# Scores of a four-layer recurrent block: three bfloat16 parts on 72 rows, loaded by head from DRAM, in place of float32 products over 128 rows

## The chip, the cores and the metric

The kernel runs on one core of a Trainium2 chip. A core has five engines that run side by side, each with its own list of instructions: TensorE (PE in the profile; its weight loads are listed apart as PEld), VectorE (DVE), ScalarE (ACT), GpSimd (POOL) and SyncE (SP), which here issues every DMA. PSUM takes the products of TensorE, SBUF holds all else on the core, DRAM lies outside. The metric is the device time of one execution in microseconds; less is better. Three runs of the kernel before took 4462.1, 4463.2 and 4484.0 us; the median is 4463.2.

## What is computed

Eight rows (batch entries) of 512 positions by 128 channels pass through four layers. Each layer is a mixing part times a gated part, added to the row. The change touches the mixing part of the last layer alone, attention with 16 heads of 8 channels, of which each query keeps its 25 strongest keys:

```python
q = _layernorm(q, q_gamma, q_beta)
k = _layernorm(k, k_gamma, k_beta)
scores = jnp.einsum('bhnd,bhmd->bhnm', q, k) / jnp.sqrt(jnp.float32(D))
aw = jax.nn.softmax(scores, axis=-1)
topk = max(1, int(N * TOPK_RATIO))          # 25 of 512
kth = jax.lax.top_k(aw, topk)[0][..., -1:]
aws = aw * (aw >= kth).astype(aw.dtype)
aws = aws / (aws.sum(-1, keepdims=True) + 1e-08)
o_s = jnp.einsum('bhnm,bhmd->bhnd', aws, v)
...
o = a * o_s + (1.0 - a) * o_l               # o_l: a linear attention over softmax(q), softmax(k)
```

## The kernel before

**Recording and planning.** The kernel does not issue its instructions as it runs through its Python code. Every call is recorded as an `Op` on a `Tape`, with what it reads and writes. When all is recorded, `Tape.order` plans: it keeps a free time for each engine and an estimated cost for each operation (`Op.cost`), and at each step takes the operation that can start first, or, of several, the one with the longest way to the end behind it (`way`). Element-wise operations recorded for POOL may be planned on DVE or the other way round, and copies recorded for ACT on DVE. `Tape.play` then issues everything in the planned order, and each engine works through its list strictly in that order. That is why the profile puts nearly all instructions on line 467. Where the plan leaves TensorE idle, it puts filler: products of zeros into the PSUM tile `nd` (line 452). Filler is issued only in states of `nd` in which it does no harm. TensorE's clock is granted by the chip and is part of the plan (`Clock`).

**Streams.** Four streams of work run over the eight rows and are interleaved: `front` (layers 0 and 1, lane A of buffers), `middle` (layer 2 and the preparation of layer 3, lane B), `find` and `weigh` (layer 3, lane C). Row b's `find` is recorded about two row periods after its `front`. In the profile a tile carries its lane's letter: `midC` is a 128x512 buffer of lane C.

**Preparation** (`Layer3.channels`). Queries and keys of a row are normalised by head and transposed, so that channels lie on partitions. The channels are stored in such an order that eight small DMAs for q and eight for k, of 32 KB each, put the heads into `qh` (128 x 4 x 512) and `kh` (128 x 2 x 512). In both, a head has eight rows of channels and a ninth: −1 in `kh`, and in `qh` zero at first (eight more DMAs from a tile of zeros) and later the query's bound. There are two pairs of `qh` and `kh`, so row b waits until row b − 2 is done.

**First pass** (`find`, `rank`). For each of 4 tiles of 128 queries and each of 16 heads, one float32 product gives 128 x 512 scores in the single PSUM bank `sc`. The weights of that product are `only_q`: a copy of a 32-row strip of `qh` into a tile that is zero elsewhere, so that the product over 128 rows adds up one head only. Four such copies (ACT) are made for every eight heads. DVE then finds the 32 largest of each row of scores in four rounds: `max` gives the 8 largest, `match_replace` takes them out. After the first round the scores are in an SBUF tile `rest` (a `midC` buffer), and the next three rounds of a tile are recorded behind the first round of the following one. ACT exponentiates what is left and sums it.

**Bounds** (`bound`). After two tiles, a half of the queries, the 25th and 26th score give each query's bound between them; it is transposed (`cT`) and written to the ninth rows of `qh` by eight DMAs.

**Second pass** (`weigh`). For a half (256 queries), 4 blocks of 128 keys and 16 heads, a float32 product of `only_k` (strips of `kh`, copied as above) and `qh` gives scores minus the bound, transposed. ACT turns what is negative into minus infinity (Prelu with a slope of 1e30) and exponentiates; a product with `vpad` (values, and ones for the sums) accumulates in `nd`. `combine` divides, adds the linear attention and writes the row's output.

Of the kernel before, what the change touches and what calls it, by code (L numbers as in the profile page):

```python
# [17 lines left out]
P = 128  # L18
# [10 lines left out]
TOPK_ROUNDS = 3  # L29
# [11 lines left out]
    FILL | {AF.Exp, AF.Tanh, AF.Prelu, AF.Square, AF.Abs},  # L41
# [24 lines left out]
class View:  # L66
# [47 lines left out]
    def box(self):  # L114

        if self.room.pool.space == bass.MemoryType.DRAM:
            return 0, P, 0, 1 << 30
        whole = View.shadows[tuple(self.room.shape)]
        first = self.at.__array_interface__["data"][0] - whole.__array_interface__["data"][0]
        row = int(np.prod(self.room.shape[1:]))  # L120
        p0, f0 = divmod(first, row)
        span = [(s * (n - 1), s) for n, s in zip(self.at.shape, self.at.strides)]
        return p0, p0 + sum(d for d, s in span if s >= row) // row, f0, f0 + sum(d for d, s in span if s < row)
# [10 lines left out]
class Op:  # L134
# [29 lines left out]
    def cost(self, engine):  # L164
# [5 lines left out]
        if engine == "tensor":  # L170
            out, stay, move = wrote[0], read[0], read[1]
            passes = 2 if stay.room.dtype == F32 else 1
# [12 lines left out]
        if engine == "sync":  # L185
            size = 4 * int(np.prod((wrote or read)[0].shape))
            return 400.0, 1300.0 + size / 175.0
# [60 lines left out]
class Tape:  # L248
# [188 lines left out]
    def play(self):  # L437
# [11 lines left out]
        for n in self.order():  # L449
# [12 lines left out]
            if any(v.room.key == key for v in wrote):  # L462
                state = 2 if op.kw["stop"] else 1
            elif any(v.room.key == key for v in read):
                state = 0
# [72 lines left out]
class Lane:  # L538
# [35 lines left out]
    def tile(self, name, shape, bufs=1):  # L574
        return self.pool.tile(list(shape), F32, tag=name + self.lane, name=name, bufs=bufs)

    def scratch(self, name, shape):
        return self.dram.tile(list(shape), F32, tag=name, name=name)
# [96 lines left out]
def together(*parts):  # L675
# [10 lines left out]
    return got  # L686

# [531 lines left out]
class Layer3:  # L1219
# [17 lines left out]
    def __init__(self, k):  # L1237
# [17 lines left out]
        self.rows, self.heads = [], []  # L1255
        for i in range(2):
            qh, kh = core.held(f"qh{i}", (P, 4, T)), core.held(f"kh{i}", (P, 2, T))
            nc.gpsimd.memset(qh, 0.0)
            nc.gpsimd.memset(kh, -1.0)
            self.heads.append((qh, kh))  # L1260
        self.only_q, self.only_k = [], []
        for to, name in ((self.only_q, "q0"), (self.only_q, "q1"), (self.only_k, "k")):
            t = core.held(f"only_{name}", (P, 4, 2, P))
            nc.gpsimd.memset(t, 0.0)
            to.append(t)
        self.Wproj = core.whole("w3p")("Wproj")

    def row(self, b):

        r = Layer3.__new__(Layer3)  # L1270
        r.__dict__.update(self.__dict__)
        r.b, r.done, r.masses = b, False, {}
        self.rows.append(r)
        return r
# [17 lines left out]
    def channels(self, k, w, xn):  # L1292
# [35 lines left out]
        heads_of = lambda t: t.rearrange("p (r d s) -> p r s d", r=8, d=D)  # L1328
        for c, name in ((0, "q"), (1, "k")):
            for t in range(NT):  # L1330
                yield
                y = raw[:, t, c * P : (c + 1) * P].rearrange("p (r s d) -> p r s d", r=8, d=D)
                vec = lambda n: row(name + n).unsqueeze(1).unsqueeze(1).to_broadcast([P, 8, 2, D])
# [6 lines left out]
        for g in range(G):  # L1340
            yield
            mine = top[:, g, :].rearrange("p (r s) -> p r s", r=8)
            nc.vector.reduce_max(mine, heads_of(QK[:, g, :]), axis=AX.X)
            nc.gpsimd.tensor_sub(
                f[:, g, :].rearrange("p (r s d) -> p r s d", r=8, d=D),
                heads_of(QK[:, g, :]),
                mine.unsqueeze(3).to_broadcast([P, 8, 2, D]),
# [8 lines left out]
        while self.b >= 2 and not self.rows[self.b - 2].done:  # L1356
            yield
        self.qh, self.kh = self.heads[self.b % 2]
        for c in range(2):
# [4 lines left out]
            zs = k.mid("qk_t")  # L1364
            nc.scalar.copy(zs, z)
            for r in range(4):
                for i in range(2):
                    at = slice(32 * r + 9 * i, 32 * r + 9 * i + D)
                    to = self.kh[at, :, :] if c else self.qh[at, 2 * i : 2 * i + 2, :]
                    nc.sync.dma_start(out=to, in_=zs[32 * r + 16 * i : 32 * r + 16 * i + 16, :])  # L1370
                    if c == 0:
                        at = slice(at.stop, at.stop + 1)
                        none = self.only_q[0][P - 1 :, 0, 0:1, :].to_broadcast([1, 8, P])
                        nc.sync.dma_start(
                            out=self.qh[at, 2 * i : 2 * i + 2, :].rearrange(
                                "p s (t n) -> p (s t) n", n=P
                            ),
                            in_=none,
                        )
# [25 lines left out]

    def find(self):
# [5 lines left out]
        for n in range(NT * H):  # L1412
            t, h = divmod(n, H)
            a, r = divmod(h, 4)
            i, s = divmod(a, 2)
            if h == 0:
                top = k.tile("top", (P, H, (TOPK_ROUNDS + 1) * 8), 2)

                each = k.tile("each", (P, 2, H), 2)
            if h % 8 == 0:  # L1420
                only = self.only_q[i]
                for at in (slice(32 * j, 32 * j + 32) for j in range(4)):
                    nc.scalar.copy(
                        only[at, at.start // 32],
                        self.qh[at, 2 * i : 2 * i + 2, t * P : (t + 1) * P],
                    )
            z = k.psum.tile([P, T], F32, tag="sc", name="sc", bufs=1)
            k.mm(z, only[:, r, s, :], self.kh[:, s, :])
            head = 4 * r + a
            mine = top[:, head, :]  # L1430
            nc.vector.max(mine[:, 0:8], z)
            rest = k.mid("rest")
            nc.vector.match_replace(rest, mine[:, 0:8], z, -3e38)
            nc.gpsimd.tensor_scalar_mul(each[:, 0, head : head + 1], mine[:, 0:1], -self.scale)
            if behind:
                self.rank(*behind)
            behind = n, head, top, each, rest
            yield
        self.rank(*behind)

    def rank(self, n, head, top, each, rest):
        k, nc, H = self.k, self.k.nc, self.H
        mine = top[:, head, :]
        for m in range(1, TOPK_ROUNDS + 1):
            best = mine[:, 8 * m : 8 * m + 8]
            nc.vector.max(best, rest)
            if m < TOPK_ROUNDS:
                nc.vector.match_replace(rest, best, rest, -3e38)
        k.act(
            rest, rest, AF.Exp, scale=self.scale,  # L1450
            bias=each[:, 0, head : head + 1], accum_out=each[:, 1, head : head + 1],
        )
        t, h = divmod(n, H)
        if h < H - 1:
            return

        large = 8 * TOPK_ROUNDS
        e_top = k.tile("exp_top", (P, H, large))
        nc.gpsimd.tensor_sub(e_top, top[:, :, 0:large], top[:, :, 0:1].to_broadcast([P, H, large]))
        k.act(e_top, e_top, AF.Exp, scale=self.scale)  # L1460
        if t % 2 == 0:
            self.marks = k.tile("marks", (P, 4, 2, H), 2)
        nc.vector.reduce_sum(self.marks[:, 3, t % 2, :], e_top, axis=AX.X)
        nc.vector.tensor_add(self.marks[:, 3, t % 2, :], self.marks[:, 3, t % 2, :], each[:, 1, :])
        for to, at in enumerate((0, 24, 25)):
            nc.gpsimd.tensor_copy(self.marks[:, to, t % 2, :], top[:, :, at])
        if t % 2:
            self.bound(t // 2)

    def bound(self, half):  # L1470
# [4 lines left out]
        m, t25, t26, mass = (self.marks[:, i] for i in range(4))  # L1475
# [20 lines left out]
        cols = slice(half * self.HALF, (half + 1) * self.HALF)  # L1496
        for r in range(4):
            for i in range(2):
                at = 32 * r + 9 * i + D
                nc.sync.dma_start(  # L1500
                    out=self.qh[at : at + 1, 2 * i : 2 * i + 2, cols],
                    in_=cT[4 * r + 2 * i : 4 * r + 2 * i + 2, 0 : self.HALF],
                )
        self.bounded = half + 1

    def weigh(self, half, out):
# [18 lines left out]
        for n in range(32):  # L1525
            c, a, lo = n // 8, n // 2 % 4, 2 * (n % 2)
            i, s = divmod(a, 2)
            if n % 8 == 0:
                only = self.only_k[0]
                for at in (slice(32 * j, 32 * j + 32) for j in range(4)):  # L1530
                    nc.scalar.copy(only[at, at.start // 32], self.kh[at, :, c * P : (c + 1) * P])

            e = k.tile("weights", (P, 2, self.HALF), 3)
            z = k.ps().rearrange("p (j q) -> p j q", j=2)
            for j in range(2):
                k.mm(z[:, j, :], only[:, lo + j, s, :], self.qh[:, a, cols])
            k.act(e, z, AF.Prelu, alpha=1e30)
            k.act(e, e, AF.Exp, scale=self.scale)
            for j in range(2):
                r = lo + j  # L1540
                k.mm(
                    nd[32 * r : 32 * r + 32, i, :], self.vpad[:, c, 2 * r + i, s, :], e[:, j, :],
                    start=False, stop=n >= 30,
# [320 lines left out]
```

## Time and profile before

| | us |
|---|---|
| three runs | 4462.1, 4463.2, 4484.0 |
| median | 4463.2 |
| profiled execution, first to last instruction | 4466.0 |
| VectorE busy in it | 3883.5 |
| TensorE busy, with 689.5 of filler (L452) | 4215.7 |
| mean granted TensorE clock | 0.962 of full speed |
| DMAs issued by SP, all engines' queues | 100560 packets, 239.16 MB, 18.1% of 16 engines |

How to read the profile's lines. A row of the groups gives line, engine, operation, written tile <- read tiles, shapes and count, then busy time in us, the mean duration of one in ns, and idle time just before them with what ended it. Busy time counts overlapping records once, so busy time divided by the count can be less than the mean. A float32 product shows as two matmul records. A row of the stages gives a stretch, its length, and for each engine the busy time and, in brackets, the number of instructions, then the granted clock, the share of the DMA engines and GB/s. A row of the waits gives who waited for whom, the total in us, how often, and the longest.

### The profile page before, as it was taken

The numbers are of one execution on the slowest core, as the hardware profiler recorded it, in microseconds if no ns is written. First come the engines' busy times: TensorE is split into PE (matmuls) and PEld (weight loads), VectorE is DVE, ScalarE is ACT, GpSimd is POOL, SyncE is SP. The second block draws the span as 40 slices with busy tenths as digits, with TensorE's granted clock in tenths as the row PEclk, the third lists the DMA queues.
The fourth block names the chain that finished last, engine by engine and source line by source line (L and its number), as shares of the span: only waits on it lengthen the run. The fifth ranks groups of instructions, "written<-read, shape, count | busy, mean of one in ns | idle before, by whom it ended". The sixth has DMA issues, their size and how long they took to land. (4 is left out here: it accounts for less than half of the span.)

```text
span 4466.0 us, 59645 instructions
## 1 busy us (share of the span) xinstructions
PE 4215.7 (94%) x19508; PEld 2096.0 (47%) x19508; DVE 3883.5 (87%) x7617; ACT 2873.1 (64%) x5883; POOL 2492.4 (56%) x2973
## 2 busy tenths in 40 slices
PE   9998899999999999999999999999999999999699
PEld 4554454445444545444445445444444444444244
DVE  5438859989989998999898999999799989999894
ACT  3434455557766786767776686767775687375355
POOL 4117736873869565874757656784479533833010
PEclk9989999999999999999999999999999999999799
DMA  3122312221122121222012220221212100200000
GB/s 94 49 54 73 93 48 66 73 87 57 52 64 84 49 55 41 77 61 77 30 50 67 71 62 29 72 83 36 60 51 84 49 23 28 74 19 17 2 5 10
DMA packets 100872, 242.97 MB, mean 54 GB/s; under 512 B 13009, under 2 KB 25425, under 8 KB 96465
## 3 DMA queue, kind: packets, MB, share of 16 engines
q1 hardware_dynamic: 100560, 239.16, 18.1%
q8 instruction: 154, 2.52, 0.2%
q14 instruction: 158, 1.29, 0.1%
HBM read 206.60 MB, written 15.20 MB: 50 GB/s over the span
## 5 line engine op out<-in xcount | busy, mean ns | idle before, releaser
L467 DVE MAX8 topC<-midC 128x8 f32<-128x512 f32 x1374 | 912.8, 683 | 2.8
L467 POOL TENSOR_TENSOR midB<-midB,midB 128x512 f32<-128x512 f32 x520 | 670.7, 1299 | 104.4 <-DVE midB L467 94.3
L452 PE MATMUL nd<-ones,zeros 128*128 128x512 bf16 (+3 forms) x2956 | 689.5, 367 | 18.2 <-ACT midC L467 16.5
L467 PE MATMUL sc<-kh,only_q 128*128 128x512 f32 x1024 | 567.4, 637 | 66.4 <-DVE midC L467 22.4
L467 DVE MATCH_REPLACE8 midC<-topC,midC 128x512 f32<-128x512 f32 x916 | 619.5, 678 | 0.0
L467 PE MATMUL psA<-midA,wA 128*128 128x512 f32 (+3 forms) x986 | 524.5, 635 | 29.8 <-ACT midA L467 6.1
L467 PE MATMUL psC<-qh,only_k 128*128 128x256 f32 x1836 | 522.1, 397 | 16.5 <-ACT weightsC L467 10.8
L452 PEld LDWEIGHTS <-zeros 128*128 128x128 bf16 x2956 | 282.6, 100 | 458.8 <-issue 217.0
L467 ACT ACTIVATE midC<-midC,eachC 128x512 f32<-128x512 f32 x458 | 329.1, 719 | 219.9 <-DVE topC L467 209.8
L467 ACT ACT_TABLE_LOAD x343 | 440.1, 1283 | 21.1 <-DVE topC L467 5.4
L467 PEld LDWEIGHTS psC<-qh,only_k 128*128 128x128 f32 x1836 | 323.7, 191 | 244.0 <-issue 105.1
L467 POOL TENSOR_SCALAR eachC<-topC 128x1 f32<-128x1 f32 x497 | 108.3, 222 | 536.6 <-DVE topC L467 495.0
L467 DVE MAX8 topC<-sc 128x8 f32<-128x512 f32 x512 | 354.1, 692 | 54.5 <-PE sc L467 52.6
L467 ACT ACTIVATE weightsC<-psC 128x512 f32<-128x512 f32 x459 | 271.4, 591 | 104.8 <-PE psC L467 66.2
L467 PE MATMUL psB<-XNB,wB 128*128 128x512 f32 x556 | 311.3, 644 | 26.8 <-DVE midB L467 24.4
L467 PE MATMUL nd<-weightsC,vpad 128*32 128x256 f32 x2048 | 314.3, 392 | 11.4 <-ACT weightsC L467 10.7
L467 ACT ACTIVATE weightsC<-weightsC 128x512 f32<-128x512 f32 x512 | 316.4, 628 | 8.1
L467 DVE MATCH_REPLACE8 midC<-topC,sc 128x512 f32<-128x512 f32 x458 | 312.6, 683 | 0.0
L467 POOL TENSOR_TENSOR midB<-wideB,midB 128x512 f32<-128x512 f32 x228 | 292.9, 1288 | 18.7 <-DVE wideB L467 11.1
L467 DVE TENSOR_TENSOR_SCAN midB<-psB,midB 128x512 f32<-128x512 f32 x236 | 285.7, 1212 | 7.5 <-ACT psB L467 6.2
L467 PEld LDWEIGHTS sc<-kh,only_q 128*128 128x128 f32 x1024 | 175.1, 194 | 237.3 <-DVE midC L467 97.5
L467 PEld LDWEIGHTS psA<-midA,wA 128*128 128x128 f32 (+3 forms) x986 | 163.9, 187 | 220.7 <-issue 96.7
(738 smaller groups left out, 8114.8 us busy)
## 6 DMA issues: line engine op xcount, KB each, us to landing
midB<-bc SPq DMA_DIRECT2D x247, 256.0 KB
wideA<-qk SPq DMA_DIRECT2D x31, 1024.0 KB
wB<-in_moe_dram SPq DMA_DIRECT2D x32, 512.0 KB
wideA<-wideA SPq DMA_DIRECT2D x30, 384.0 KB
wA<-in_rope_q_dram SPq DMA_DIRECT2D x16, 512.0 KB
wA<-in_w1k_dram SPq DMA_DIRECT2D x16, 512.0 KB
wA<-in_w1v_dram SPq DMA_DIRECT2D x16, 512.0 KB
wB<-in_moed_dram SPq DMA_DIRECT2D x32, 256.0 KB
```

Source lines behind the costliest of these rows:

```text
L452: made = nc.tensor.matmul(slots[key][0].rearrange("p i (j n) -> p (i j) n", n=64)[:, 0 : -n // 64, :], real(zeros), real(ones).unsqueeze(1 ...
L467: made = getattr(getattr(nc, op.by), how)(*map(real, op.args), **{k: real(x) for k, x in op.kw.items()})
```

## The change

It replaces the float32 products of both passes by bfloat16 ones, and with them the way in which heads get to the array:

- **Three parts.** The transposed q and k are split into three bfloat16 numbers each (`split`: copy, subtract, copy, subtract, copy, recorded for POOL), whose sum is the float32 value. All nine products of parts of 8 channels make 72 rows.
- **By way of DRAM.** The parts are written to a DRAM scratch (`stackq` with three copies of each part, nine DMAs; `stackk` with one, three DMAs), ordered by head. There are three such scratches, and no wait for row b − 2. `stack` loads 72 rows of one head back: 72x256 for q, and for k the 24 rows of all 512 keys, repeated three times.
- **First pass.** It runs over halves of the queries and heads, with two products of 128 queries for each load. Three pairs of tiles, `find_q` and `find_k`, take turns. `max` and `match_replace` stay as they were: `BEST` = 8 in the first round and `FOLDED` = 24 in the three that follow.
- **Second pass.** For each half and head it loads 72 rows of q and of k into `weigh_q` and `weigh_k` (three of each), and the three parts of the bound, from `bound_parts`, into three more rows of q, which meet −1 in k. The loop runs over heads outside and key blocks inside.
- **Gone** are `qh`, `kh`, `only_q`, `only_k`, all copies into them and the DMAs that filled them. The channels of a head lie side by side (`heads_of`).
- Lane C has 6 `mid` buffers in place of 4. The planner costs a bfloat16 product at half of a pass in place of a whole one, and the size of a DMA by its type. In `play`, the state of `nd` stays "done" after the first product that is marked as a last one, where before it went back with the next that is not.

```diff
+def split(k, parts, whole):
+    nc = k.nc
+    for i in range(PARTS):
+        nc.gpsimd.tensor_copy(parts[:, i, :], whole)
+        if i < PARTS - 1:
+            nc.gpsimd.tensor_sub(whole, whole, parts[:, i, :])
...
-            zs = k.mid("qk_t")
-            nc.scalar.copy(zs, z)
-            for r in range(4):
-                for i in range(2):
-                    at = slice(32 * r + 9 * i, 32 * r + 9 * i + D)
-                    to = self.kh[at, :, :] if c else self.qh[at, 2 * i : 2 * i + 2, :]
-                    nc.sync.dma_start(out=to, in_=zs[32 * r + 16 * i : 32 * r + 16 * i + 16, :])
...
+            whole = k.tile("qk_t", (P, T))
+            nc.scalar.copy(whole, z)
+            parts = k.tile("parts", (P, PARTS, T), dtype=BF16)
+            split(k, parts, whole)
+            copies = 1 if c else PARTS
+            spill = k.scratch("stack" + "qk"[c], (H, PARTS, copies, D, T), BF16, 3)
+            for i in range(PARTS):
+                for j in range(copies):
+                    nc.sync.dma_start(out=spill[:, i, j], in_=parts[:, i, :])
+            self.stacks.append(spill)
...
+    def stack(self, to, side, h, cols):
+        rows = self.stacks[side][h, :, :, :, cols].rearrange("i j d n -> (i j d) n")
+        if side:
+            rows = rows.unsqueeze(0).to_broadcast([PARTS, PARTS * self.D, cols.stop - cols.start])
+        self.k.nc.sync.dma_start(out=to[0:STACK, 0 : cols.stop - cols.start], in_=rows)
...
-        for n in range(NT * H):
-            t, h = divmod(n, H)
...
-            if h % 8 == 0:
-                only = self.only_q[i]
-                for at in (slice(32 * j, 32 * j + 32) for j in range(4)):
-                    nc.scalar.copy(
...
-            k.mm(z, only[:, r, s, :], self.kh[:, s, :])
+        for n in range(2 * H):
+            half, h = divmod(n, H)
+            cols = slice(half * self.HALF, (half + 1) * self.HALF)
+            q, kk = self.find_q[n % 3], self.find_k[n % 3]
+            self.stack(q, 0, h, cols)
+            self.stack(kk, 1, h, slice(0, T))
+            q, kk = q[0:STACK, :], kk[0:STACK, :]
...
+            for t in range(2):
+                z = k.psum.tile([P, T], F32, tag="sc", name="sc", bufs=1)
+                k.mm(z, q[:, t * P : (t + 1) * P], kk[:, 0:T])
...
+        self.bounds[half] = k.tile("bound_parts", (H, PARTS, self.HALF), 2, BF16)
+        split(k, self.bounds[half], cT[:, 0 : self.HALF])
...
-        for n in range(32):
-            c, a, lo = n // 8, n // 2 % 4, 2 * (n % 2)
...
+        for at in range(self.H):
+            a, r = divmod(at, 4)
...
+            q, kk = self.weigh_q[at % 3], self.weigh_k[at % 3]
+            self.stack(q, 0, h, cols)
+            nc.sync.dma_start(out=q[STACK : STACK + PARTS, :], in_=self.bounds[half][h : h + 1])
+            self.stack(kk, 1, h, slice(0, T))
+            q, kk = q[0 : STACK + PARTS, :], kk[0 : STACK + PARTS, :]
+            for n in range(2):
+                e = k.tile("weights", (P, 2, self.HALF), 3)
+                z = k.ps().rearrange("p (j q) -> p j q", j=2)
+                for j in range(2):
+                    c = 2 * n + j
+                    k.mm(z[:, j, :], kk[:, c * P : (c + 1) * P], q)
...
-    third = Lane(core, "C", mid=4, wide=0, weights=0, banks=1)
+    third = Lane(core, "C", mid=6, wide=0, weights=0, banks=1)
```

## The prediction

> **What bounds the kernel now.** I read the head of the page first, then busy time in three stages, then the waits of VectorE in the middle stage, then the groups that the change touches.
>
> ```profile
> span 4466.0 us, 59645 instructions
> ...
> PE 4215.7 (94%) x19508; PEld 2096.0 (47%) x19508; DVE 3883.5 (87%) x7617; ACT 2873.1 (64%) x5883; POOL 2492.4 (56%) x2973
> ...
> DVE  5438859989989998999898999999799989999894
> ```
>
> TensorE looks fullest, but L452 on it is filler. So I cut the span where the first score product starts and where the layers before the attention run out (670 and 4019 us), and set the filler beside it: first the three stages, then L452 alone in the middle one.
>
> ```profile
> 0.00:670.00 670.00, 623.84 (x3195) 317.96 (x3196) 413.77 (x584) 292.88 (x643) 286.12 (x272) 0.94 0.23 68
> 670.00:4019.00 3349.00, 3207.04 (x14612) 1590.43 (x14611) 3119.15 (x6235) 2357.88 (x4777) 2151.93 (x2555) 0.97 0.20 58
> 4019.00:4466.00 447.00, 384.86 (x1704) 187.62 (x1701) 350.60 (x799) 222.35 (x465) 54.32 (x147) 0.93 0.03 8
> ```
> ```profile
> 670.00:4019.00 3349.00, 371.06 (x1589) 149.49 (x1590) 0.97 0.20 58
> ```
>
> The columns after the length are PE, PEld, DVE, ACT, POOL. In the middle PE has 3207 − 371 = 2836 us of real work (85%), DVE 3119 of 3349 (93%). DVE is the tighter one. It idles 670 − 414 = 256 us in the head, 230 in the middle, 447 − 351 = 96 in the tail: 582 in all, and 3883.5 + 582 is the span. I forecast by these four terms. What ends DVE's idle time in the middle:
>
> ```profile
> DVE topC L467 <- PE sc L467: 36.2, 44, 3.8
> DVE wideA L467 <- ACT midA L467: 19.1, 21, 4.1
> DVE midC L467 <- ACT midC L467: 19.0, 21, 2.4
> DVE att_smallA L467 <- PE psA L467: 18.5, 14, 5.5
> ```
>
> Summed over that whole view, PE ends 109 us, ACT 83, POOL 13, DMA 9.
>
> **The change, part by part.** *Products.* These are the old products, the filler as nearest row for bf16, and the top-k on DVE:
>
> ```profile
> L467 PE MATMUL sc<-kh,only_q 128*128 128x512 f32 x1024 | 567.4, 637 | 66.4 <-DVE midC L467 22.4 <-DVE midA L467 16.1 <-DMA qh<-midB 15.1
> L467 PE MATMUL psC<-qh,only_k 128*128 128x256 f32 x1836 | 522.1, 397 | 16.5 <-ACT weightsC L467 10.8
> L452 PE MATMUL nd<-ones,zeros 128*128 128x512 bf16 x2458 | 614.0, 386 | 17.5 <-ACT midC L467 15.8 <-DVE ones L467 1.0 <-ACT midA L467 0.7
> L452 PE MATMUL nd<-ones,zeros 128*128 128x256 bf16 x52 | 14.7, 283 | 0.0
> L467 DVE MAX8 topC<-midC 128x8 f32<-128x512 f32 x1374 | 912.8, 683 | 2.8
> ```
>
> An f32 product is two records. Find has 512: 567.4/512 = 1.108 us each; a bf16 one of 512 columns takes 614.0/2458 = 0.250, which saves 512 × 0.858 = 439 us of PE. Weigh has 1024 of 256 columns: psC, psA and psB together (522.1 + 34.2 + 22.7)/1024 = 0.565; bf16 is 0.283 by the 52 short fillers, half of 0.250 at best. I take 0.283, as it has the same shape: 1024 × 0.282 = 289 (at best 450). A change of the array's shape can take some back: in the last chain a lone psA product takes 0.63 us where two in a row take 0.86, so 0.2 per change, 512 × 0.2 = 102 in find. PE saves 728 us, bounds 626 and 889. None is taken off the span as such: what it is worth is DVE waits.
>
> *Top-k.* DVE still does four MAX8 and three MATCH_REPLACE8 on every one of 512 score tiles; the rounds are renamed, none is dropped. The built program has 6084 instructions on DVE, 6083 before. Gone are 24 copies into only_q and 30 into only_k (0.284 us: 15 us). Added are 11 of the split's steps (about 0.69 us: 8) and a few small shifts: DVE 3880.
>
> *ACT* loses 458 copies into only_q and only_k, 92.9 + 90.5 = 183 us, and 343 − 294 = 49 table loads at 1.283 = 63. It is 70% busy in the middle; this only shortens waits.
>
> *The split* (copy, subtract, on POOL by preference): in the built order 41 copies and 28 subtractions of 512 columns on POOL, 41 × 0.70 + 28 × 1.30 = 65 us, and 77 short ones on 16 rows for the bounds, under 0.74 each: at most 57. Covered by POOL's 36% idle in the middle; without that cover it is 120 us over eight rows, 15 a row, late for the first heads of a row.
>
> *Transfers.* 2071 instead of 1015. The queue's issue cost before:
>
> ```profile
> L467 SPq DMA_DIRECT2D qh<-midC x128: 558/559/1637, 660.6 to 4395.2; - x128
> L467 SPq DMA_DIRECT2D midB<-bc x247: 319/320/1271, 391.8 to 3911.1; - x124
> ```
>
> New: 1024 loads of stacks, 256 of bounds, 96 spills at 0.32 to 0.67 us; gone: 320 at about 0.62. Net 1376 × 0.5 − 198 = 490 us of SP, which is then about a quarter issued. A stack load may start when the product three heads back has read its buffer; DVE needs two tiles × (4 × 0.60 + 3 × 0.67 + 3 × 0.08 = 4.65 us), near 9 us, for a head, so there are 18 us for a load that took 1.6 to 2.3 us from issue to use in the last chain (qh<-midB). Cost nothing, hidden by DVE; a load that SP holds behind another wait for over 15 us is late, and sc, then DVE, wait for it. Bounds: 0 and, with every head as late as the longest such wait before (5.5 us), 256 × 5.5.
>
> The Trainium skill speaks against these loads ("DMA: Bandwidth & Descriptors", "Why a DMA increments its semaphore by 16"): such a DMA uses the largest number of engines up to 16 that divides the outer size on both sides, so the key stack, repeated three times, would sit on three. By the page's rule and the mean packet of the trace (18.1% of 16 × 4466 us over 100560: 0.129 us) that is 24 × 0.129 = 3.1 us in place of 0.6 for a spread one: still inside the 18 us, and 10 us more at the very end. I leave it out of the sum; no row of before shows it.
>
> *Head.* Row 0's chain from its transposed q to the first score was 24 DMAs from 661.5 to 676.7, 15 us. The new one: five split steps (0.7 and 1.3: 4.7), nine writes, landing, load, landing: 12 to 15 us; if the nine writes to one scratch wait for each other, 9 × 2.3 = 21 and some 10 to 15 more. I take +6: 262. Later rows are covered by the backlog of scores.
>
> *Middle.* Of 230 us: the sc waits (36) go, as the product gets 0.86 us shorter; midC <- ACT midC (19) goes, with six buffers for four; waits for only_q and only_k (15) go with the copies. Of the other PE-ended 65 I take half, as PE's real work falls from 85% to some 66%; of the other ACT-ended 64 an eighth. Left 230 − 36 − 19 − 15 − 32 − 8 = 120. Bounds: 230 (nothing gained) and 60.
>
> *Tail.* The last pass of weigh:
>
> ```profile
> 4393.00:4455.00 62.00, 55.54 (x311) 34.01 (x311) 8.41 (x20) 40.73 (x78) 0.00 (x0) 1.00 0.01 3
> ```
>
> PE is 90% busy there, ACT 66%. With PE relieved ACT sets it: 32 × (0.59 + 0.63) = 39, near 42 with its edges: −20. The split of the bounds in front of it adds 3 to 4: 96 − 16 = 80, bounds 65 and 100.
>
> **Sum:** 3880 + 262 + 120 + 80 = 4342 on the profile's 4466.0. That execution lies 2.8 above the median 4463.2: 4340 us, 2.8% less.
>
> **The clock.** PE's speed follows its load in this trace (PE busy first, clock third from the end):
>
> ```profile
> 4180.00:4200.00 20.00, 10.38 (x10) 2.51 (x10) 16.62 (x46) 0.00 (x0) 0.00 (x0) 0.50 0.00 0
> 4220.00:4240.00 20.00, 14.76 (x56) 6.11 (x56) 13.32 (x25) 4.82 (x13) 0.35 (x2) 0.73 0.03 8
> ```
>
> The middle would hold about 2836 − 620 = 2216 us of work in 3240 (68%), plus filler, of which the new order has as much as the old (2931 pieces for 2956): near 80%. At a clock of 0.85 the work grows to 2216 × 0.97/0.85 = 2530, still under DVE.
>
> The skill's "TensorE: Matmul & The Clock Gate" (What's actually happening) halves the clock only after a whole idle window of about 3.4 us. By that rule the middle stays at 0.97 and the sum stands at 4340.
>
> By the rows, 0.73 at 74% busy, PE's steps in the middle could take 0.97/0.73 = 1.33 times as long: the half of the 65 us that I gave to PE is then not gained (32), and the 65 last a third longer (21), which makes 4393. The rows decide: this is the upper end of the forecast's own range.
>
> **Rivals.** (1) *The waits move but do not shrink:* DVE still idles 230 us in the middle, since what it awaits are chains of dependent steps over PE and ACT, and a wait taken away shows up at the next link. For it: the 230 are spread over many pairs, the largest of them 36 us; PE was not the only full engine. Against: the sc and midC waits, whose causes go. Head +6, tail −16: 4463 − 10 = 4453, no change. (2) *Late stack loads, slower:* SP takes its entries in order, and its waits before were up to 122 us long (ACT midC), so a load may stand behind one whose time has slipped. Each us late per head costs 256 us; it decides from (4463 − 4340)/256 = 0.48 us on. At the mean of the four only_q waits for qh (7.4/4 = 1.85) on half the heads: 4340 + 237 = 4577. Against: DMA ends only 9 us of DVE's waits. (3) *DVE fills almost wholly:* one stretch of 223 us already reaches 98.5% (219.74, from 2903 to 3126); the middle at 98% gives 60 idle: 4280.
>
> **How the numbers follow.** Forecast 0.60 (own range 4295 to 4400), rival 3 0.15, rival 1 0.12, rival 2 0.13. Half a per cent, 22 us, is what a measurement here tells from no change: 4441 and 4485. Faster: 0.60 + 0.15 + 0.03 of rival 1 = 0.78; same: 0.09 of rival 1 and 0.01 of rival 2 = 0.10; slower: 0.12 of rival 2. The range runs from rival 3's 4280 less 25, as its head and tail have bounds too, to 4465, which takes in rival 1 and leaves out rival 2.
>
> **What would show it.** DVE busy 3880 ± 15 and idle near 460; DVE's waits for sc in the middle under 15 us; PE without filler near 2800; the last pass of weigh near 42 us, ACT over 85% busy in it; find products about 0.25 to 0.45 us. Wrong if DVE waits behind sc, and sc behind a DMA into find_q or find_k; if PE's clock in the middle is under 0.8; or if DVE's busy time itself moves by over 40 us.

## The result and the profile after

The changed kernel takes 4495.7 us (median of 12 runs, 4481.0 to 4510.4), the kernel before on the same chip 4474.4 (12 runs, 4462.1 to 4484.0). The ratio is 1.0052, 95% interval 1.0037 to 1.0067: slower by half a per cent, where 2.8% less was forecast and the range ended at 4465. The profile, with a span of 4479.2 us, is of the shortest of the twelve.

The head of the page and the granted clock in 40 slices:

```profile
span 4479.2 us, 57690 instructions
...
PE 3856.7 (86%) x17947; PEld 1808.3 (40%) x17947; DVE 3873.5 (86%) x7618; ACT 2628.0 (59%) x5368; POOL 2553.4 (57%) x2970
...
PEclk9989999999889889988999799989989978696887
```

TensorE has lost 359 us of busy time and ScalarE 245, VectorE 10. Yet the span grew by 13. The clock, 0.962 before, is 0.891. The three stages, cut as before (length; then PE, PEld, DVE, ACT, POOL; clock third from the end), and the filler alone in the middle one:

```profile
0.00:670.00 670.00, 630.12 (x3239) 324.87 (x3240) 400.77 (x584) 298.11 (x649) 282.05 (x264) 0.95 0.24 70
670.00:4019.00 3349.00, 2945.95 (x13458) 1371.64 (x13458) 3099.01 (x6191) 2137.70 (x4316) 2221.76 (x2570) 0.89 0.25 74
4019.00:4479.20 460.20, 280.61 (x1253) 111.81 (x1251) 373.69 (x844) 192.19 (x403) 49.58 (x136) 0.78 0.10 29
```
```profile
670.00:4019.00 3349.00, 403.71 (x1727) 163.00 (x1727) 0.89 0.25 74
```

VectorE idles 269 us in the head (forecast 262), 250 in the middle (120), 86 in the tail (80), and is busy 3873 (3880). So 130 of the 137 us between 4479 and the sum of 4342 lie in one term: the middle's idle time, which was to be halved and grew by 20. What ends it:

```profile
DVE midA L472 <- PE psA L472: 44.1, 47, 2.9
DVE topC L472 <- PE sc L472: 33.4, 48, 2.1
DVE wideA L472 <- ACT midA L472: 26.5, 28, 3.6
DVE att_smallA L472 <- PE psA L472: 23.2, 11, 6.1
...
DVE midC L472 <- ACT midC L472: 3.9, 5, 1.2
```

Over the whole view PE ends 144 us (before 109), ACT 81 (83), POOL 7 (13), DMA 3 (9). Two entries were to go. The one for midC has gone, from 19.0 to 3.9, with the two more buffers. The one for the score tile has not: 36.2 became 33.4, though its product is 0.7 us shorter. And waits for products that the change doesn't touch, psA above all, grew. The groups:

```profile
L472 PE MATMUL nd<-weightsC,vpad 128*32 128x256 f32 x2048 | 497.2, 400 | 22.1 <-ACT weightsC L472 19.7
L472 PE MATMUL sc<-find_k,find_q 72*128 72x512 bf16 x512 | 216.8, 424 | 183.1 <-DVE midC L472 147.1 <-DVE midB L472 18.4 <-DVE midA L472 11.4
L472 PE MATMUL psC<-weigh_q,weigh_k 75*128 75x256 bf16 x918 | 194.3, 284 | 15.5 <-ACT weightsC L472 11.3 <-ACT massC L472 2.7 <-ACT midC L472 0.3
```

The score products save what was forecast: 567.4 − 216.8 = 351 us in the first pass and, over psA, psB and psC, 573.6 − 213.5 = 360 in the second, 711 against 728. But TensorE's work without filler fell only from 3526 to 3173 us, by 353. Two things took the rest back. The products with the values, nd<-weightsC, not edited at all, went from 314.3 to 497.2 (+183). And 711 − 183 − 353 = 175 us are left by which all other work got dearer, at a lower clock (the run e1 below shows that most of it is the clock). On PE's timeline one sees it (start, duration, operation; idle time before it in brackets):

```profile
2003.20 1.02 PE L472 MATMUL psB<-wideB,wB 128*128 128x512 f32 x2
2004.06 0.38 PE L472 MATMUL sc<-find_k,find_q 72*128 72x512 bf16 x1
2015.35 2.05 PE L472 MATMUL psA<-midA,center 128*128 128x512 f32 x2 [10.91 <-DVE midA L472]
2018.56 0.58 PE L472 MATMUL sc<-find_k,find_q 72*128 72x512 bf16 x1 [1.17 <-DVE midC L472]
```

PE stands still for 10.9 us with no filler in the gap. The psA product after it takes 2.05 us, where two records of this size took 1.02 before the gap, the next score product 0.58 for 0.38.

### The profile page after: what moved, and what is told of

It reads as the page before. It is cut to its first block, busy times and chain, and to the rows that moved or that the text cites. A ratio compares the mean times of both kernels' runs of the same rounds, so it can differ in the third digit from the quotient of the medians.

```text
span 4479.2 us, 57690 instructions
## 1 busy us (share of the span) xinstructions
PE 3856.7 (86%) x17947; PEld 1808.3 (40%) x17947; DVE 3873.5 (86%) x7618; ACT 2628.0 (59%) x5368; POOL 2553.4 (57%) x2970
## 5 line engine op out<-in xcount | busy, mean ns | idle before, releaser
L472 DVE MAX8 topC<-midC 128x8 f32<-128x512 f32 x1386 | 897.9, 679 | 1.9
L472 POOL TENSOR_TENSOR midB<-midB,midB 128x512 f32<-128x512 f32 x533 | 684.0, 1292 | 151.3 <-DVE midB L472 144.2
L457 PE MATMUL nd<-ones,zeros 128*128 128x512 bf16 (+6 forms) x2931 | 683.9, 366 | 20.5 <-ACT midC L472 15.2
L472 PE MATMUL nd<-weightsC,vpad 128*32 128x256 f32 x2048 | 497.2, 400 | 22.1 <-ACT weightsC L472 19.7
L472 PE MATMUL psB<-XNB,wB 128*128 128x512 f32 x556 | 343.7, 706 | 84.0 <-DVE midB L472 76.3
L472 PE MATMUL sc<-find_k,find_q 72*128 72x512 bf16 x512 | 216.8, 424 | 183.1 <-DVE midC L472 147.1
L472 PEld LDWEIGHTS nd<-weightsC,vpad 128*32 128x32 f32 x2048 | 157.3, 111 | 249.6 <-issue 93.6
L472 ACT ACTIVATE psB<-wideB,neg_a 128x512 f32<-128x512 f32 x240 | 165.8, 691 | 155.8 <-DVE midB L472 130.2
L472 ACT ACTIVATE midA<-psA,vec 128x512 f32<-128x512 f32 (+3 forms) x226 | 153.7, 683 | 135.8 <-PE psA L472 131.2
```

The source lines that it names most:

```text
L457: made = nc.tensor.matmul(slots[key][0].rearrange("p i (j n) -> p (i j) n", n=64)[:, 0 : -n // 64, :], real(zeros), real(ones).unsqueeze(1 ...
L472: made = getattr(getattr(nc, op.by), how)(*map(real, op.args), **{k: real(x) for k, x in op.kw.items()})
```

## The experiments

Each ratio is to the kernel before, run beside it on the same chip.

### Filler and strips

Counted in the plan, the new order calls for 5180 pieces of filler and issues 2931; the old one called for 3100 and issued 2956. The rest is left out because the state of `nd` says "done" from the first product marked as a last one until the sums are read, and now the last blocks of four heads carry that mark.

**e1_close_last:**

```diff
-                        start=False, stop=a == 3 and c == NT - 1,
+                        start=False, stop=False,
...
+        _, zeros, ones = nc.filler
+        for r in range(4):
+            k.mm(
+                nd[32 * r : 32 * r + 32, 1, :].rearrange("p (j n) -> p j n", n=64), zeros[:, 0:32],
+                ones.unsqueeze(1).to_broadcast([P, self.HALF // 64, 64]), start=False, stop=True,
+            )
```

> The changed kernel, but nd is closed by four small zero products at the end of each half instead of by the products of the last four heads; so filler may be issued until then. Of the planned filler, 4781 pieces of 5185 are issued (the changed kernel: 2931 of 5180; before: 2956 of 3100). Clock theory (the filler that was left out let TensorE's clock fall from 0.96 to 0.89, and slower float32 steps of the other layers make VectorE wait): clock back to 0.95 or more, VectorE idle in the middle from 250 to about 150 us, time about 0.98 of before (4380 us beside 4474). Strip theory (the products into nd now queue on one 32-column strip and cost 183 us more of TensorE): nd stays at 400 us or more, time 1.00 to 1.005 of before. Chain theory (VectorE's waits are chains of dependent steps, whatever TensorE does): clock may rise, idle stays at 600 us in all, ratio 1.005.

Measured: 4456.3 us, ratio 0.9956 (0.9936 to 0.9977), with 4781 pieces. The middle stage of e1, and its filler alone:

```profile
670.00:4019.00 3349.00, 3173.35 (x15218) 1492.37 (x15218) 3129.55 (x6258) 2135.20 (x4339) 2232.15 (x2581) 0.96 0.26 75
```
```profile
670.00:4019.00 3349.00, 770.30 (x3360) 320.89 (x3361) 0.96 0.26 75
```

The clock is back at 0.96 with 770 us of filler for 404, and the same products cost TensorE 155 us less over the whole run: 3018 us without filler for 3173. VectorE idles 219 us, not 120: the clock was a part only.

**e2_before_nofill** is the kernel before without its filler (`if False:` for `if state < 2:` in `play`), the same measured from the other side.

> The kernel before with its planned order unchanged and no filler issued at all (2956 pieces left out, 690 us of TensorE's busy time). Clock theory: mean clock below 0.88, float32 products of the layers longer, VectorE's idle time up, and the time up by 1% or more (4520 us or more). Chain theory: time within 0.5% of before.

Measured: ratio 1.0244 (1.0202 to 1.0285, from two runs), clock 0.879 for 0.962, and PE ends 169 us of VectorE's waits in the middle for 109. The planned order is the same here, so this is the worth of filler by itself.

**e4_pairs** puts the second pass's loop back towards the old order, two heads at a time with the key blocks inside, so that products with the values which follow each other go to different strips of 32 columns:

```diff
-        for at in range(self.H):
-            a, r = divmod(at, 4)
+        for pair in range(self.H // 2):
+            a, lo = pair // 2, 2 * (pair % 2)
...
-            for n in range(2):
+            for c in range(NT):
```

> The changed kernel with weigh going over pairs of heads, key blocks inside, so that neighbouring products into nd go to different strips as before; six buffers of weigh_q and weigh_k; filler as in the change (3234 of 5445 pieces issued). Clock theory: clock stays below 0.91, ratio to before 0.995 to 1.005. Strip theory: nd<-weightsC from 497 to about 320 us busy and the time down by 1% or more, ratio 0.98 to 0.995. Chain theory: nd shorter, ratio 1.005 as for the change.

Measured: ratio 0.9975 (0.9955 to 0.9995). Two such products on PE's timeline, in the changed kernel and in e4:

```profile
1527.48 1.05 PE L472 MATMUL nd<-weightsC,vpad 128*32 128x256 f32 x4
```
```profile
1517.16 0.63 PE L472 MATMUL nd<-weightsC,vpad 128*32 128x256 f32 x4
```

Four records take 1.05 us to one strip and 0.63 to two; the group falls from 497.2 to 362.6 us, with a record as long as before (402 ns for 400).

(The tiles of its stacks are six for three.) **e5_pairs_close_last** has both edits.

> Both: pairs of heads and nd closed at the very end (4996 of 5403 pieces of filler issued). Clock theory: like e1_close_last, ratio about 0.98, and at most 0.5% better than it. Strip theory alone: like e4_pairs. Both theories: ratio 0.97 to 0.975, the 4340 us that were forecast. Chain theory: 1.005.

Measured: 4409.0 us, ratio 0.9867 (0.9827 to 0.9908). Its middle stage, and the filler alone:

```profile
670.00:4019.00 3349.00, 3159.08 (x15497) 1474.77 (x15496) 3147.43 (x6309) 2140.62 (x4349) 2232.67 (x2592) 0.95 0.26 75
```
```profile
670.00:4019.00 3349.00, 834.26 (x3645) 345.56 (x3644) 0.95 0.26 75
```

TensorE's real work in the middle is 3159 − 834 = 2325 us (69%), near the 66% of the forecast, for 2836 before. Yet of the 202 us that VectorE idles, PE ends 110, as many as in the kernel before.

### Work and loads

If the rest is TensorE's load, adding or taking work must show. All four kernels start from e5.

**e6_e5_find_twice** issues `k.mm(z, q[:, t * P : (t + 1) * P], kk[:, 0:T])` twice.

> The kernel of e5 (pairs of heads, closing products), with each product of the first pass issued twice into the same scores: 512 products of about 0.40 us more, some 203 us of TensorE work. Is the TensorE time that the change saves worth anything once strips and clock are mended? By the forecast's step (TensorE's load sets VectorE's waits; 728 us saved were to end 36 + 32 us of them) 203 us more give back some 19 us of the 110 that TensorE ends in e5's middle, and the time goes from e5's 4409 to about 4428, ratio to before 0.991. By the chain theory (a wait is the length of a chain of dependent steps) only the waits for the score tile can grow, 48 of them by 0.4 us, and the ratio stays at 0.987 within 0.002.

Measured: 4339.0 us, ratio 0.9713 (0.9683 to 0.9743). Neither theory: with 512 products more than e5 it is 70 us *faster*.

**e7_e5_half_weigh** skips two of four key blocks (`if c % 2: continue`).

> The kernel of e5 with two of the four key blocks of the second pass left out (its products, its Prelu and Exp, its products with the values): TensorE loses about 94 + 174 us, ScalarE about 512 x 1.2 / 2 = 310 us, VectorE nothing. Load theory: waits that TensorE and ScalarE end in e5's middle (110 and 69 us) fall by a third or more, 60 us, and the tail by 20: 4409 - 80 = 4330. Chain theory: only the tail gains, some 20 to 25 us, the middle's idle time stays at 200 within 15: about 4385.

Measured: 4447.9 us, ratio 0.9951 (0.9935 to 0.9968). With 262 us less of ScalarE it is *slower* than e5, and PE still ends 139 us of VectorE's waits in the middle. Both theories miss. (A second draw of e5, e21 below, has the ratio 0.9928, so against e5 this run says only that no gain came.)

**e8_e5_loads_once** puts `if self.b == 0 and n < 3:` before the loads of find, and the like before those of weigh.

> The kernel of e5 with the loads of stacks and bounds left out but for the first three heads of find and the first six of weigh, so that later heads work on the first ones' data: 1024 + 256 DMAs of SyncE are gone but for some 24. If late loads, SyncE's list or the transfers' traffic hold VectorE up (the forecast's rival 2), the middle's idle time falls by 40 us or more: 4370 or less. If loads are hidden, as the trace of the changed kernel suggests, the time stays at e5's 4409 within 15 us.

Measured: 4421.7 us, ratio 0.9888 (0.9864 to 0.9912). Some 1250 DMAs fewer gain nothing (the two draws of e5 have 0.9867 and 0.9928): the loads are hidden.

**e11_e5_rows128** drops `q, kk = q[0:STACK, :], kk[0:STACK, :]`, and the like in weigh, and zeroes the tiles once.

> The kernel of e5 with all stacks used over 128 rows, the rows above 72 (75) being zero in the queries: products of the same shape as their neighbours and the filler, where e5's have 72 rows. If the change of the array's shape is what makes the first pass's product last 0.40 us in place of the 0.25 of a filler of 512 columns, the product falls to 0.25 to 0.30 and TensorE's work by 50 to 75 us. The time: by the chain theory within 10 us of e5's 4409, by the load theory 5 to 10 us less.

Measured: ratio 0.9843 (0.9810 to 0.9877). The product of the first pass in it:

```profile
L472 PE MATMUL sc<-find_k,find_q 128*128 128x512 bf16 x512 | 200.3, 391 | 42.7 <-DVE midC L472 28.1 <-DVE midB L472 8.7 <-DVE midA L472 4.2
```

391 ns for e5's 396: not the array's shape. A record of the filler is as long (386 ns); the filler's 0.250 each comes from records that overlap, and this product stands alone.

### The plan

e6 and e7 also changed what the planner had to place, so the next runs changed the plan alone.

**e14_e6_order_once** plans e6, but issues without the second products:

```diff
                 k.mm(z, q[:, t * P : (t + 1) * P], kk[:, 0:T])
+                k.mm(z, q[:, t * P : (t + 1) * P], kk[:, 0:T])
+                nc.ops[-1].left_out = True
...
+            if getattr(op, "left_out", False):
+                continue
```

> The kernel of e6 planned with both copies of the first pass's product, but issued without the second ones: the order of all that remains, and the filler, are e6's. If e6's gain lies in the order alone, this is as fast as e6 (ratio 0.971 within 0.003, or a little faster, as 512 products of 0.40 us are gone). If the added products themselves helped (a clock that they hold, spacing on TensorE), it is slower than e6, towards e5's 0.987.

Measured: 4329.9 us, ratio 0.9672 (0.9653 to 0.9691), 3.3% less than before. The same instructions as e5 apart from filler and placement (which engine takes a step), 79 us less: the plan alone. Its stages, the middle stage of e6, and the wait for scores in e14 and, below it, in e6:

```profile
670.00:4019.00 3349.00, 3069.27 (x14942) 1418.42 (x14940) 3163.21 (x6376) 2155.52 (x4394) 2271.85 (x2709) 0.95 0.26 76
4019.00:4328.70 309.70, 201.07 (x1030) 78.73 (x1029) 259.95 (x591) 145.18 (x317) 23.17 (x75) 0.82 0.09 29
```
```profile
670.00:4019.00 3349.00, 3151.58 (x15443) 1466.17 (x15442) 3163.86 (x6384) 2159.18 (x4399) 2275.71 (x2713) 0.96 0.26 76
```
```profile
DVE topC L474 <- PE sc L474: 7.5, 12, 1.9
```
```profile
DVE topC L472 <- PE sc L472: 21.7, 38, 2.4
```

With the order held fixed, the second products cost TensorE 166 us (the group is 368.7 us in e6 and 203.0 in e14, as two in a row overlap), and the waits for scores grow by 14. But in the middle, where TensorE's work without filler is 2470 us in e6 (682 are filler) and 2381 in e14 (689), VectorE idles 185 us in e6 and 186 in e14, of which PE ends 86 and 89: other waits shrank by as much. So the forecast's mechanism, less work on TensorE and hence fewer waits, shows in the one wait and not in the sum. The medians are 9 us apart; the plan is worth several times as much.

**e12_after_full_pass** undoes one line of the change, the planner's cost:

```diff
-            passes = 2 if stay.room.dtype == F32 else 0.5
+            passes = 2 if stay.room.dtype == F32 else 1
```

> The changed kernel with one part undone: the planner costs a bfloat16 product at a whole pass again (430 ns for a product of the first pass, 215 for one of the second) in place of half a pass (215 and 108); measured they take 424 and 284. Nothing that is computed changes, only the planned order. Theory 'plan': issuing the find product twice made e5 faster by 70 us because the planned time of the step then came near the measured one, so the order fits the chip better; the changed kernel should gain in the same way, to 4430 or less (ratio 0.990 or less). Theory 'chance': the order's quality varies by some per cent with any small change of the plan and has nothing to do with the cost; the ratio stays within 0.998 to 1.012.

Measured: 4428.5 us, ratio 0.9896 (0.9875 to 0.9917): 1.6% less than the changed kernel, with every product as it was.

**e13_e5_full_pass**, the same on e5:

> The same on e5 (pairs of heads, closing products): a bfloat16 product planned at a whole pass. Theory 'plan': as e6, about 4340, ratio 0.97, and fewer instructions on VectorE, more on GpSimd (e6: 7541 and 3049, e5: 7617 and 2974). Theory 'chance': between 0.975 and 0.997, without a leaning to e6.

Measured: ratio 0.9808 (0.9783 to 0.9833). Between, and no shift of work from VectorE (7622 instructions) to GpSimd (2977).

**e16_after_find_pass** plans the first pass's product alone at a whole pass (`1 if stay.shape[0] == STACK else 0.5`).

> The changed kernel, in which the planner costs the first pass's products alone at a whole pass (430 ns; measured 424), all else at half. If the planned time of this product is what spoils the order, the ratio is near e12's 0.990 (0.985 to 0.995). If e12's gain was a draw, it lies anywhere in 0.990 to 1.012.

Measured: ratio 0.9909 (0.9875 to 0.9942).

### How much is the draw

A plan of many thousand steps may turn on a nanosecond. A draw, in what follows, is one such plan out of the many that small changes give. `SLACK` is added to every planned end and changes nothing but the order. **e15_before_slack5**, the kernel before:

> The kernel before, with 5 ns added to every operation's planned end (SLACK = 5 in place of 0), which reorders the plan here and there and changes nothing else. It measures how much the time depends on the plan by chance. If the time is smooth in the plan's constants, the ratio is 1.000 within 0.003. If before's order is one fortunate draw of many, it is slower by up to 1 to 2%, and part of what the change lost is the loss of that draw.

Measured: ratio 0.9966 (0.9948 to 0.9984): another draw of before is a third of a per cent better, so nothing says that before's order was a lucky one.

**e17_after_slack2** and **e18_after_slack5**, the changed kernel with 2 and 5 ns:

> The changed kernel with 2 ns on each planned end: another draw of its plan, with its too low costs. Theory 'plan': it stays slow, 1.005 within 0.004, since the costs are as wrong as before. Theory 'chance': it can land as low as e12's 0.990.

> The changed kernel with 5 ns on each planned end: a third draw. The same as for e17_after_slack2: 1.005 within 0.004 by the theory 'plan', anything down to 0.990 by the theory 'chance'.

Measured: 1.0079 (1.0059 to 1.0099) and 1.0002 (0.9983 to 1.0020). None of the three draws comes near 0.990. The half per cent by which the changed kernel is slower lies within these draws; the 2.8% of gain that was forecast lies far outside.

**e19_e14_slack5**, **e20_e5_find_pass** (pairs, closing products and e16's cost) and **e21_e5_slack5**:

> The kernel of e14 (e6's order without the second products) with 5 ns on each planned end: the same mended costs, strips and closing products, another draw. If e14's 0.967 comes from what was mended, the ratio stays within 0.004 of it; if it is a fortunate draw, it goes back towards e13's 0.981.

> The kernel of e5 in which the planner costs the first pass's products alone at a whole pass: pairs of heads, closing products and cost mended, no products added or left out. By the sum of the three causes (1.004 for the mean of the changed kernel's three draws, less 0.018 for e5 and 0.014 for the cost) 0.972, within 0.007, as e13, e14 and e19 spread (0.967 to 0.981). If the three don't add, 0.981 or more.

> The kernel of e5 with 5 ns on each planned end: a second draw of it. If strips and clock are worth what e1, e4 and e5 showed, the ratio stays at 0.987 within 0.005; at 0.996 or more, much of e5's gain was a draw.

Measured: 0.9737 (0.9720 to 0.9755), 0.9776 (0.9753 to 0.9798), 0.9928 (0.9905 to 0.9952). All draws together:

| ratio to before | first pass's product planned at half a pass | at a whole pass |
|---|---|---|
| the changed kernel | 1.0052, 1.0079, 1.0002: mean 1.0044 | 0.9896, 0.9909: mean 0.9903 |
| with pairs and closing products | 0.9867, 0.9928: mean 0.9898 | 0.9808, 0.9672, 0.9737, 0.9776: mean 0.9748 |

(e14 and e19 reach the whole pass with two products planned at half; e12 and e13 raise the second pass's cost too.) Each mending is worth 1.4 to 1.6% between the means of a row or a column, where draws lie at most 0.8% from their mean, and no draw of one cell reaches into the next of its row or column. In the last cell only e13 and e20 edit the cost itself; their mean is 0.9792, and by it each mending is worth 1.1% there. What e14 and e19 have beyond that comes from plans with phantom products, which are planned and never issued. e1 and e4 are one draw each and not far from e18's 1.0002; in the middle they idle 219 and 233 us, the three draws of the changed kernel 250, 238 and 228. That filler and strips matter to TensorE's work is shown by their rows, the share of each in the 1.5% isn't. And e21, the second draw of e5, idles 237 us in the middle, of which PE ends 157. The best kernel is e14, 3.3% below before; a plain version without the phantom products, e20, is 2.2% below.

## Why the prediction was wrong

**Right:** VectorE bounds; its busy time (3873 for 3880), head and tail (269 and 86 for 262 and 80), ScalarE's loss (245 for 246), the last pass of weigh (from 4420.5 to 4458.3, 38 us for 42, though with PE busy for 89% of it and ScalarE for 78, not over 85), the midC waits, hidden loads (rival 2 falls with e8), and the sum of the score products (711 for 728). That sum is right by luck: the first pass saved 351 us for 439, as its product stands alone at 0.42 us and not 0.25, and the second 360 for 289. A small misreading cost nothing: in the room for a load the prediction takes 0.60 us for a MAX8, where the row that it shows has 912.8/1374 = 0.66.

**The step that failed** is the middle: "the sc waits (36) go" and "Of the other PE-ended 65 I take half, as PE's real work falls from 85% to some 66%". The sc waits stayed (33), though the product got shorter by 0.68 us; the other PE-ended ones rose to 111 in place of falling to 33; ACT's other waits were 77 for 56, midC kept 4, and POOL ended 6 less: 33 + 78 + 21 + 4 − 6 = 130, the 130 us that were missed. Two things went wrong in it. Real work fell only to 2542 of 3349 (76%). And the waits do not follow the work: in e5 it is down to 69% and PE ends 110 us (157 in e21), for 109 before the change at 85%; e6 and e14, of one order, differ by 89 us of TensorE's work in the middle and not in its idle time. That less load on TensorE would halve those waits was assumed, and no run bears it out. Beside this, the prediction priced three terms at nothing or not at all:

1. *Filler*, "of which the new order has as much as the old". As many pieces, yes, but 353 us less work needs more of them, and the rule for the state of `nd` kept 2249 back. The prediction weighed the clock and put its cost at +53 us at most. e1 shows the clock come back with the pieces, and with it 155 us of TensorE's work.
2. *The loop order of the second pass*, not mentioned: 183 us of TensorE from products that the diff leaves alone. e4 gives 135 of them back. Terms 1 and 2 together are worth 1.5% at the change's planner cost.
3. *The planner's cost of a bfloat16 product*, in the diff and in the text, and priced nowhere: 1.4% on the changed kernel (e12, e16), 1.1% on e5 (e13, e20).

With the three mended the mean is 0.975 (0.979 without the plans with phantom products), and the forecast was 0.972. That isn't the forecast borne out: e14 has 3821 us of VectorE work (7541 instructions, 77 fewer than the changed kernel, with 79 more on GpSimd), 272 + 186 + 50 of idle time. It gets there by placing and by a short tail, and its middle still idles 186 us, not 120.

**Rival 1**, a wait that moves to the next link, was nearest: in e5, with clock and strips mended, PE ends 110 us of waits and in e21 157, no fewer than before the change. It was given 4453; the two terms of clock and strips and the planner's cost put the time above that. The chance of slower was all on rival 2, which was not what happened.

**What stays open:** why a whole pass plans better. One score product and its reader on the changed kernel's timeline:

```profile
1557.75 0.39 PE L472 MATMUL sc<-find_k,find_q 72*128 72x512 bf16 x1
...
1558.18 0.70 DVE L472 MAX8 topC<-sc 128x8 f32<-128x512 f32 x1
```

VectorE begins 0.43 us after the product's start. The plan's end at half a pass is 0.215 + 0.165 + a hop of 0.035 (what the planner adds from one engine to the next) = 0.415, about right at full clock; at a whole pass it is 0.63. So the better plan is the one with 0.2 us to spare, or with TensorE taken for as long as the 0.42 that it is (half a pass takes it for 0.215). No run separates these. Nor do the gains lie in one place: against the changed kernel, e16 has 23 us less VectorE work, 26 less idle time in the middle and 13 in the tail; e12 17 us more work and 51 less idle in the middle. The waits for sc themselves are 36.5 us in e16 and 25.1 in e12, for 33.4.

## What to carry to other kernels

Where a planner writes the order, its cost table is part of the change: price the edit of a cost as a draw of the whole order, and run two or three draws (a nanosecond on each planned end) before a difference of a per cent or so is believed (here draws of one kernel lay up to 0.8% apart). A loop turned inside out also reorders the products that it doesn't edit; look at which neighbours used to overlap. And when work is taken off an engine whose clock follows its load, ask what keeps the load up, and whether the rule that lets the filler in still holds.

## What the hardware showed that was not expected

**The clock falls after windows in which TensorE was busy.** The middle of the changed kernel has 65 periods at half clock, 707 us (before: 31, 201 us), in steps of 3.41 us. Here are three such steps at full clock, each with the one after it (PE busy, then the clock):

```profile
2004.42:2007.83 3.41, 0.02 (x1) 1.00 0.51 154
2007.83:2011.25 3.42, 0.00 (x0) 0.50 0.00 0
1331.99:1335.41 3.42, 1.27 (x6) 1.00 0.15 50
1335.41:1338.82 3.41, 3.41 (x12) 0.50 0.00 0
1400.26:1403.67 3.41, 3.21 (x12) 1.00 0.04 13
1403.67:1407.08 3.41, 1.78 (x4) 0.50 0.23 77
```

Only 4 of the 65 follow a step with under 0.1 us of PE records; half follow one with over 2 us, 13 one that was full; the mean is 1.99 us of 3.41. The Trainium skill's "TensorE: Matmul & The Clock Gate" (What's actually happening) gives the half rate after at least one idle window of about 3.4 us. The window and the two rates agree with this trace, the condition doesn't, if idle is read as a window without busy records: busy time in the records can't be all that the gate goes by. What it goes by wasn't tried.

**Products on different strips overlap.** Four float32 records into 32 columns each take 1.05 us on one strip and 0.63 on two, each record lasting 0.40 either way.
